# A recommender's attention over 200 history rows: more embedding rows fetched by address, asked four steps ahead, and VectorE empties the first layer's PSUM

## The chip, the cores and the metric

The kernel runs on one core of a Trainium2 chip. The metric is device time in microseconds for one launch. Engines carry the profile's names: PE (TensorE), DVE (VectorE), ACT (ScalarE), POOL (GpSimd) and SP (SyncE); SPq, ACTq and POOLq are their queues, which issue DMAs.

## What is computed

The reference, cut to what matters (B = 16384 samples, L = 200 history entries, embeddings of D = 64 floats, tables of 100,000 rows, hidden width A = 36):

```python
it = i_emb[item]                       # [B, 64]
h = i_emb[hist]                        # [200, B, 64]
feat = concatenate([h, itb, h - itb, h * itb], axis=-1)
a = dice(feat @ au_W1 + au_b1, au_alpha, axis=1)   # moments over B, for each l
w = a @ au_W2 + au_b2
cur = sum(w * h, axis=0)
z = concatenate([u, it, c, cur])       # then a small head of three layers
```

`dice(x)` is `x * (p + alpha * (1 - p))` with `p` the sigmoid of `x` normalized by its mean and variance over the batch. So for each of 200 values of l, 16,384 rows of 256 bytes are fetched from a table in HBM, put through a small layer, and the layer's output can be gated only when its moments over the whole batch are known.

## The kernel before

**Tiles and steps.** The batch is 128 tiles of P = 128 samples. Eight columns of TD = 16 tiles make up one l; one column is one step, so the main part has 1,600 steps, numbered k = 8 l + c. The loop body (L580) holds 90 l written out and runs twice; the last 20 l and the head follow. All engine orders are written out by hand (`manual_schedule`): each engine executes its instructions in program order and waits on semaphores.

**How rows come.** Most tiles come by `gather` (L123): one indirect DMA issued by POOL fetches 128 rows by a column of ids in SBUF. Three tiles of each l, the last tile of columns 3, 5 and 7 (`SIDES`, L27), come "by address" instead: their ids are loaded into one partition (`load_addresses`, L136), scaled to byte offsets by DVE (`scale_addresses`, L139), and SP and ACT fetch them into registers, up to LOAD = 28 at a time (L326), and issue one 256-byte DMA for each row (`row_by_address`, L290) into one of BUFS = 6 side buffers. These row DMAs are called asks here. The 384 rows of an l are spread evenly over its eight steps, 24 on SP and 24 on ACT in each (`shares`, L304; `ask_hist`, L343). When a column is due, DVE waits on the buffer's semaphore, clears it (`await_rows`, L349) and copies the tile to its place in the column (`place`, L384; `place_tile`, L390). Gathered columns go into a ring of ROWS = 5 buffers, so POOL can run up to four steps ahead of DVE.

**One step** (`step`, L435) works on several columns at once: rows of column k are fetched (L358); column k-1 is turned, by four DVE transposes into hT (L149), and multiplied on PE into the PSUM tiles ph and px (`turn`, L406; `product`, L411, where DVE forms hm = ph * itT); column k-2 leaves px for xs with the bias added (`hidden`, L376, on ACT), and DVE takes its batch statistics (`measure`, L379); column k-9 is gated on ACT (`gate`, L364: pg from xs, with the scale and shift of its l), DVE multiplies pg by xs into y and PE forms wb (`weights`, L368), and DVE weighs hT by it and adds to curT (`weigh`, L372). Every eighth step the moments of an l are finished (`moments`, L415) right after its last column's statistics, ahead of that step's transposes. All of DVE's work of a step stands in one order: statistics and moments, place, transposes, measure, hm, y, wb, curT. PE's order is ph, px, px from hm, wb. px has one buffer: the next step's px matmuls wait until hidden has read it.

**ACT's queue** in a step: hidden, the asks (24, in one load), gate. **SP's queue**: the id loads (L131), the address load at column 2 of an l for the next l, and its 24 asks in each step; it has nothing else and runs ahead until a side buffer or an address table isn't free. Addresses are scaled by DVE at column 4.

**Before the loop** (L526 to L577) the item rows are gathered, category rows are picked by matmuls, and the head's weights are loaded by SP at c = 2 (`head_weights`, L242), with a wait of DVE for them. **After it** (L664 on) user rows are fetched while the last columns are weighed, two of their tiles by address, and the head's layers follow.

Of the kernel before, what the change touches and what calls it, by code (L numbers as in the profile page):

```python
# [15 lines left out]
P = 128  # L16
# [5 lines left out]
LPB = 90  # L22
ROWS = 5
# [3 lines left out]
SIDES = (3, 5, 7)  # L27
BUFS = 6
# [7 lines left out]
def din_kernel(  # L36
# [80 lines left out]
    addrs = make("addrs", 2 * S + 1, NS * P, dt=I32)  # L117
    addr = [addrs[i * S : i * S + 1] for i in range(3)]
# [160 lines left out]
    keys = {}  # L279

    def tiles_by_address(l):

        return l * NS, range(NS)
# [30 lines left out]
    def ask(queue, runs, first, tiles, at, table):  # L314
# [6 lines left out]
        for r0, end in runs:  # L321
            while r0 < end:
                many = end - r0
                while place_of(r0 + many - 1) != place_of(r0) + many - 1:
                    many -= 1
                _, loaded = nc.values_load_multi_w_load_instructions(  # L326
                    at[:, place_of(r0) : place_of(r0) + many],
                    engines=(engine,), min_val=0, max_val=ROW * (table.shape[0] - 1),
                    skip_runtime_bounds_check_because="scale_addresses holds the address to the table",
                )  # L330
                for r, a in enumerate(loaded, r0):
                    m, p = first + r // P, r % P
                    key = keys.setdefault(m, f"rows{next(serial)}")
                    dma = row_by_address(
                        queue,
                        side[m % BUFS].bitcast(U8)[p : p + 1],
                        flat[ds(a, ROW)].rearrange("(o d) -> o d", o=1),
                    ).then_inc(landed[m % BUFS], 16)
# [4 lines left out]
    def ask_hist(k, queue, some):  # L343
        l, s = divmod(k, ND)
        first, tiles = tiles_by_address(l)
        runs = shares(len(tiles) * P // ND, s, SPLIT)[queue]
        ask(queue, runs[some], first, tiles, addr[l % 3], i_emb)

    def await_rows(m):  # L349
        if m in keys:  # L350
            fence = nc.vector.wait_ge(landed[m % BUFS], 16 * P)
            tc.declare_fence(fence.ins, group=keys.pop(m))
            nc.vector.sem_clear(landed[m % BUFS])

    def has_side(k):
        return k % ND in SIDES

    def fetch(k):  # L358
        l, c = divmod(k, ND)
        for n in range(TD - has_side(k)):  # L360
            j = column(c, n)
            gather(rows[k % ROWS], idx[l % IDX][:, j : j + 1], n, i_emb)
# [13 lines left out]
    def hidden(k):  # L376
        nc.scalar.activation(xs[k % XR], px, AF.Identity, bias=au_bias)  # L377
# [57 lines left out]
    def step(k, last=None, weighed=()):  # L435
# [30 lines left out]
    def steps(l0, n, end, then=None):  # L466
        for k in range(n * ND):
# [58 lines left out]
    with tc.manual_schedule():  # L526
# [19 lines left out]
        for c in range(ND + 1):  # L546
# [8 lines left out]
            if c == 0:  # L555
                attention_weights()
                load_hist_ids(0, 0)
                load_addresses(0, r_hist[0:1])
                scale_addresses(0)
            if c == 2:  # L560
# [9 lines left out]
        for t in (*hT[:SPREAD], *side, curT[0], rows[-1 % ROWS]):  # L570
# [5 lines left out]
        for c in range(1, 2 * ND):  # L576
            nc.vector.tensor_copy(stats[-1 % 3][:, c, :], stats[-1 % 3][:, 0, :])  # L577

    if BODY:
        with tc.For_i(0, BODY, LPB) as l0:  # L580
# [83 lines left out]
    with tc.manual_schedule():  # L664
# [4 lines left out]
        tiles = [SIDES.index(c) for c in (3, 5) if c in SIDES]  # L669
# [131 lines left out]
```

## Time and profile before

| | |
|---|---|
| Median of 3 runs | 31,650.93 us (31,650.28 to 31,652.98) |
| The profiled execution | 31,646.96 us, its span 31,645.1 us |
| Mean granted TensorE clock | 0.806 |
| Busy share of the span | POOL 75%, PE 66%, DVE 49%, PE weight loads 27%, ACT 12% |
| Asks for history rows | 38,400 on SP, 38,400 on ACT |
| Gathers for history rows | 25,000 on POOL |

How to read it: busy shares count instructions of the engine itself. A queue that only issues DMAs, or fetches addresses into registers, isn't busy by this count; such work is seen in the timelines, as rows of SPq and ACTq, and in a line's or tile's own view. In a group's row the first number after the bar is busy time, then the mean length of one in ns, then the idle time ahead of these instructions and what ended most of it. A row of a timeline has its start, its length (both in us) and how many instructions it merges; in brackets stands the idle time ahead of it. A row of the stage table has the stretch, its length, busy time and count of PE, PE's weight loads, DVE, ACT and POOL, then granted clock, DMA share and GB/s.

### The profile page before, as it was taken

How to read it: one execution, taken by the hardware profiler on the slowest of the kernel's cores; microseconds unless marked ns; L12 is line 12 of the kernel's file. 1: busy time of each engine (PE TensorE's matmuls, PEld its weight loads, DVE VectorE, ACT ScalarE, POOL GpSimd, SP SyncE). 2: the span in 40 equal slices, each digit the busy share in tenths (PEclk: the TensorE clock that was granted, in tenths of full speed). 3: DMA queues.
4: the chain of work that ended last, by engine and by line, in shares of the span. 5: the costliest groups of instructions: out<-in, count | busy, mean ns of one | idle time of the engine just before them, and what ended most of it. 6: DMA issues, size and time to landing. Idle time of an engine off the chain costs nothing.

```text
span 31645.1 us, 223489 instructions
## 1 busy us (share of the span) xinstructions
PE 20823.3 (66%) x39536; PEld 8584.9 (27%) x39536; DVE 15548.7 (49%) x21275; ACT 3817.4 (12%) x3322; POOL 23853.6 (75%) x25259
## 2 busy tenths in 40 slices
PE   6666666666666666666666666666666666666666
PEld 2222222222222222222222222222222222222222
DVE  5444444444444444444444444444444444444445
ACT  1111111111111111111111111111111111111111
POOL 7777777777777777777777777777777777777776
PEclk8888788887888888888788888887878788887888
DMA  2111111111111111111111111111111111111111
GB/s 44 28 28 28 28 28 28 28 28 28 28 28 28 28 28 28 28 28 28 28 28 28 28 28 28 28 28 28 28 28 28 28 28 28 28 28 28 28 28 30
DMA packets 1008142, 894.16 MB, mean 28 GB/s; under 512 B 597358, under 2 KB 597559, under 8 KB 1006695
## 3 DMA queue, kind: packets, MB, share of 16 engines
q0 software_dynamic: 808128, 829.14, 15.0%
q1 hardware_dynamic: 114362, 27.92, 0.4%
q10 hardware_dynamic: 84205, 22.70, 0.3%
q14 instruction: 1136, 9.31, 0.1%
q8 instruction: 311, 5.10, 0.1%
HBM read 873.48 MB, written 4.39 MB: 28 GB/s over the span
## 4 chain that ended last, share of the span: by engine, by line
POOL 30%; issue 11%; PE 6%; DMA 5%; DVE 2%; DVEq 0%; ACT 0%; POOLq 0%; ACTq 0%
POOL rows L124 30%; DMA rows<-in_L_rec_i_emb,idx 5%; PE px L154 3%; PE ph L154 2%; PE wb L154 2%; DVE hT L149 1%; DVE wb L373 1%; DVE curT L374 0%; DVE st L382 0%; DVEq L149 0%; DVE mv L418 0%; DVE rows L392 0%; DVE addrs L141 0%; POOLq L124 0%; PE pg L154 0%
## 5 line engine op out<-in xcount | busy, mean ns | idle before, releaser
L124 POOL DMA_INDIRECT rows<-in_L_rec_i_emb,idx x25000 | 23591.6, 944 | 7633.1 <-issue 7166.6
L154 PE MATMUL ph<-hT,unit 128*128 128x512 f32 x6404 | 5969.6, 1088 | 10697.5 <-DVE hT L149 10697.5
L373 DVE SCALAR_TENSOR_TENSOR wb<-wb,au_bias,hT 128x1024 f32<-128x1024 f32 x1609 | 2079.7, 1293 | 10748.4 <-PE wb L154 10748.4
L149 DVE STREAM_TRANSPOSE hT<-rows 64x512 f32<-64x512 f32 x6404 | 4518.5, 706 | 2971.8 <-DMA rows<-in_L_rec_i_emb,idx 2529.3
L154 PEld LDWEIGHTS ph<-hT,unit 128*128 128x128 f32 x6404 | 1796.1, 311 | 13756.3 <-DVE hT L149 13561.4
L154 PE MATMUL px<-hT,blk_h 128*128 128x512 f32 x6404 | 4065.3, 723 | 0.0
L377 ACT ACTIVATE xs<-px,au_bias 128x1024 f32<-128x1024 f32 x1602 | 1784.1, 1114 | 14492.6 <-PE wb L154 14492.5
L366 ACT ACTIVATE pg<-xs,sh,rs 128x1024 f32<-128x1024 f32 x1609 | 1943.3, 1208 | 12967.9 <-issue 10092.6
L154 PE MATMUL px<-itT,blk_i 128*128 128x512 f32 x6404 | 3382.0, 610 | 0.0
L154 PE MATMUL wb<-y,blk_p 128*128 128x512 f32 x6436 | 3291.1, 593 | 11.3 <-DVE y L369 11.3
L154 PE MATMUL wb<-xs,blk_x 128*128 128x512 f32 x6436 | 3289.2, 593 | 2.6 <-DVE curT L374 2.6
L154 PE MATMUL px<-hm,blk_m 128*128 128x512 f32 x6408 | 3011.3, 592 | 0.0
L412 DVE TENSOR_TENSOR hm<-ph,itT 128x1024 f32<-128x1024 f32 x1601 | 1960.4, 1224 | 1934.9 <-PE ph L154 1934.9
L154 PEld LDWEIGHTS px<-hT,blk_h 128*128 128x128 f32 x6404 | 1627.8, 254 | 2406.1 <-issue 2304.8
L382 DVE BATCH_NORM_STATS2 st<-xs 128x6 f32<-128x512 f32 x3204 | 2058.4, 684 | 44.5 <-ACT pg L366 0.3
L369 DVE TENSOR_TENSOR y<-pg,xs 128x1024 f32<-128x1024 f32 x1609 | 1955.7, 1215 | 85.0 <-ACT pg L366 82.9
L374 DVE TENSOR_TENSOR curT<-wb,curT 128x1024 f32<-128x1024 f32 x1609 | 1969.8, 1224 | 54.8
L154 PEld LDWEIGHTS px<-itT,blk_i 128*128 128x128 f32 x6404 | 1404.8, 219 | 2000.0 <-issue 2000.0
L154 PEld LDWEIGHTS wb<-y,blk_p 128*128 128x128 f32 x6436 | 1224.5, 190 | 1551.8 <-issue 1537.2
L154 PEld LDWEIGHTS wb<-xs,blk_x 128*128 128x128 f32 x6436 | 1224.3, 190 | 1541.4 <-issue 1538.0
L154 PEld LDWEIGHTS px<-hm,blk_m 128*128 128x128 f32 x6408 | 1219.0, 190 | 1531.4 <-issue 1524.2
L124 POOL DMA_INDIRECT rows<-in_L_rec_i_emb,ids x125 | 139.7, 1118 | 39.6 <-issue 37.2
(180 smaller groups left out, 1779.3 us busy)
## 6 DMA issues: line engine op xcount, KB each, us to landing
side<-in_L_rec_i_emb SPq DMA_DIRECT2D x38400, 0.2 KB
side<-in_L_rec_i_emb ACTq DMA_DIRECT2D x38400, 0.2 KB
rows<-in_L_rec_i_emb,idx POOLq DMA_INDIRECT x25000, 2.5
idx<-in_r_hist SPq DMA_DIRECT2D x200, 62.5 KB
hT<-cs ACTq DMA_DIRECT2D x16, 500.0 KB
ucT<-catT SPq DMA_DIRECT2D x8, 512.0 KB
side<-in_L_rec_u_emb SPq DMA_DIRECT2D x256, 0.2 KB
addrs<-in_r_hist SPq DMA_DIRECT2D x200, 1.5 KB
```

Of the source, the lines that this page charges most:

```text
L124: nc.gpsimd.indirect_dma_start(out=dst[:, n, :], out_offset=None, in_=table, in_offset=bass.IndirectOffsetOnAxis(ap=ids, axis=0),)
L149: nc.vector.transpose(by_tile(dst[ts(e, D)], i)[:, n], of[ts(i, D), n, ts(e, S)])
L154: nc.tensor.matmul(dst[:, ts(i, CH)], lhsT, rhs[:, ts(i, CH)], start=(first and j == 0), stop=(last and j == len(pairs) - 1), skip_group_c ...
L366: nc.scalar.activation(pg, xs[k % XR], AF.Sigmoid, bias=shifts[i], scale=rstds[i])
L369: nc.vector.tensor_mul(y, pg, xs[k % XR])
L373: nc.vector.scalar_tensor_tensor(wb, wb, au_bias2, hT[k % LAG], ALU.add, ALU.mult)
L374: nc.vector.tensor_add(curT[k % ND], wb, curT[k % ND])
L377: nc.scalar.activation(xs[k % XR], px, AF.Identity, bias=au_bias)
L382: nc.vector.bn_stats(stats[l % 3][:, 2 * c + i, :], xs[k % XR][:, ts(i, CH)])
L412: nc.vector.tensor_mul(hm, ph, itT[k % ND])
```

## The change

1. `SIDES` becomes (1, 2, 3, 4, 5, 6, 7), with column 2 only in each fifth l: 6 tiles by address in four l, 7 in the fifth, 6.2 on average. SP and ACT each ask 48 rows a step (two loads of 24), 56 in the fifth l (two of 28). Of the other four l, column 2's last tile is gathered, with ids from a small tile `sidx` of its own.
2. Side buffers go from 6 to 9. The rows that were asked in step k are now those of step k + 4 (`LEAD`), over the ends of the loop body too: at its end and before it, DVE waits until what has been asked of the next l has landed (`hold`). The address load moves from column 2 to 0, the scaling from 4 to 3 (896 addresses instead of 384). The first four steps' rows, 384, are asked on SP before the loop, at c = 1, and the loads of user ids and head weights move behind them, to c = 8.
3. `hidden` moves from ACT to DVE. In DVE's order it stands first in a step, behind the curT of the step before, ahead of moments, place and transposes. ACT's queue in a step is now: a load of 24 or 28 asks, gate, a second load of 24 or 28.

```diff
+LEAD = 4
-SIDES = (3, 5, 7)
-BUFS = 6
+SIDES = (1, 2, 3, 4, 5, 6, 7)
+SOMETIMES = 2
+EACH = 5
+BUFS = 9
...
+    def load_side_ids(i, l):
+        j = column(SOMETIMES, TD - 1)
+        nc.sync.dma_start(sidx[i], r_hist[ds(l, 1), j * P : (j + 1) * P].rearrange("l p -> p l"))
...
-        return l * NS, range(NS)
+        first = l * (NS - 1) + l // EACH
+        return first, [j for j, c in enumerate(SIDES) if has_side(l * ND + c)]
...
+    def land(m):
+        fence = nc.vector.wait_ge(landed[m % BUFS], 16 * asked[m])
+        tc.declare_fence(fence.ins, group=keys.pop(m))
...
     def await_rows(m):
         if m in keys:
-            fence = nc.vector.wait_ge(landed[m % BUFS], 16 * P)
-            tc.declare_fence(fence.ins, group=keys.pop(m))
-            nc.vector.sem_clear(landed[m % BUFS])
+            land(m)
+        elif m not in held:
+            return
+        held.discard(m)
+        asked.pop(m)
+        nc.vector.sem_clear(landed[m % BUFS])
+
+    def hold(l):
...
+        for m in sorted(keys):
+            land(m)
+            held.add(m)
 
     def has_side(k):
-        return k % ND in SIDES
+        l, c = divmod(k, ND)
+        return c in SIDES and (c != SOMETIMES or l % EACH == EACH - 1)
...
     def hidden(k):
-        nc.scalar.activation(xs[k % XR], px, AF.Identity, bias=au_bias)
+        nc.vector.tensor_scalar(xs[k % XR], px, au_bias, None, ALU.add)
...
-        if has(k):
-            ask_hist(k, 0, slice(None))
-            ask_hist(k, 1, slice(0, 1))
+        asks = has(k) and k + LEAD < until
+        if asks:
+            ask_hist(k + LEAD, 0, slice(None))
+            ask_hist(k + LEAD, 1, slice(0, 1))
         if k - LAG not in weighed:
             gate(k - LAG)
-        if has(k):
-            ask_hist(k, 1, slice(1, None))
+        if asks:
+            ask_hist(k + LEAD, 1, slice(1, None))
...
-            if c == 2 and (l + 1 < end or then is not None):
+                if (l + 1) % EACH < EACH - 1:
+                    load_side_ids((l + 1) % IDX, l0 + l + 1)
+            if c == 0 and (l + 1 < end or then is not None):
                 load_addresses((l + 1) % 3, r_hist[ds(l0 + l + 1, 1)] if l + 1 < end else then)
-            if c == 4 and (l + 1 < end or then is not None):
+            if c == 3 and (l + 1 < end or then is not None):
                 scale_addresses((l + 1) % 3, i_emb if l + 1 < end else u_emb)
-            step(k)
+            step(k, until=end * ND)
...
-            if c == 2:
+            if c == 1:
+                for j in range(LEAD):
+                    for share in range(2):
+                        ask_hist(j, share, slice(None), 0)
+            if c == ND:
                 nc.sync.dma_start(ids[1], columns(r_user))
                 load_all_ids(1, r_user)
                 head_weights()
...
                 await_rows(tiles_by_address(LPB)[0] - 1)
+                hold(LPB)
```

More of the change, by code (lines that the diff above doesn't have):

```diff
@@ L117, in din_kernel @@
     addrs = make("addrs", 2 * S + 1, NS * P, dt=I32)
+    sidx = [make(f"sidx{i}", P, 1, dt=I32) for i in range(IDX)]
     addr = [addrs[i * S : i * S + 1] for i in range(3)]
@@ L361, in fetch @@
             j = column(c, n)
-            gather(rows[k % ROWS], idx[l % IDX][:, j : j + 1], n, i_emb)
+            ids = sidx[l % IDX] if j >= NC else idx[l % IDX][:, j : j + 1]
+            gather(rows[k % ROWS], ids, n, i_emb)
     def gate(k):
@@ L569, in din_kernel @@
             nc.scalar.copy(t, hm)
-        for t in (*hT[:SPREAD], *side, curT[0], rows[-1 % ROWS]):
+        for t in (*hT[:SPREAD], side[-1 % BUFS], curT[0], rows[-1 % ROWS]):
             nc.vector.memset(t, 0.0)
```

19 lines of the change are left out of this document (14 added, 5 removed).

## Prediction, made before the changed kernel was run

> **What bounds the kernel now.** I read the page first (span, busy times, costliest groups), then the stage table, then the timelines of single engines inside the loop.
>
> ```profile
> span 31645.1 us, 223489 instructions
> L124 POOL DMA_INDIRECT rows<-in_L_rec_i_emb,idx x25000 | 23591.6, 944 | 7633.1 <-issue 7166.6
> L149 DVE STREAM_TRANSPOSE hT<-rows 64x512 f32<-64x512 f32 x6404 | 4518.5, 706 | 2971.8 <-DMA rows<-in_L_rec_i_emb,idx 2529.3
> L373 DVE SCALAR_TENSOR_TENSOR wb<-wb,au_bias,hT 128x1024 f32<-128x1024 f32 x1609 | 2079.7, 1293 | 10748.4 <-PE wb L154 10748.4
> L377 ACT ACTIVATE xs<-px,au_bias 128x1024 f32<-128x1024 f32 x1602 | 1784.1, 1114 | 14492.6 <-PE wb L154 14492.5
> ```
> ```profile
> 185.00:14230.00 14045.00, 9236.00 (x17283) 3815.22 (x17281) 6892.02 (x9400) 1681.65 (x1450) 10613.84 (x11249) 0.80 0.16 28
> ```
>
> POOL is only 75% busy, but its idle time is "issue": it waits for nothing, each of its 25,000 gathers simply costs 944 ns and 0.3 us to the next. The stage table says it in one number: 11,249 gathers in 14,045 us, 1.2486 us each. POOL is the bound, without a pause. DVE is second: its transposes wait 2,529 us for rows.
>
> ```profile
> 200.08 2.88 DVE L149 STREAM_TRANSPOSE hT<-rows 64x512 f32<-64x512 f32 x4
> ...
> 10292.71 2.88 DVE L149 STREAM_TRANSPOSE hT<-rows 64x512 f32<-64x512 f32 x4 [1.46 <-DMA rows<-in_L_rec_i_emb,idx]
> ...
> 10297.99 1.23 DVE L412 TENSOR_TENSOR hm<-ph,itT 128x1024 f32<-128x1024 f32 x1 [1.07 <-PE ph L154]
> 10299.13 1.21 DVE L369 TENSOR_TENSOR y<-pg,xs 128x1024 f32<-128x1024 f32 x1
> 10306.57 1.29 DVE L373 SCALAR_TENSOR_TENSOR wb<-wb,au_bias,hT 128x1024 f32<-128x1024 f32 x1 [6.23 <-PE wb L154]
> 10307.90 1.23 DVE L374 TENSOR_TENSOR curT<-wb,curT 128x1024 f32<-128x1024 f32 x1
> 10313.19 2.88 DVE L149 STREAM_TRANSPOSE hT<-rows 64x512 f32<-64x512 f32 x4 [4.07 <-DMA rows<-in_L_rec_i_emb,idx]
> ...
> 31410.76 2.88 DVE L149 STREAM_TRANSPOSE hT<-rows 64x512 f32<-64x512 f32 x4 [1.30 <-DMA rows<-in_L_rec_i_emb,idx]
> ```
>
> One step is a chain through DVE and PE: transposes, PE's ph and px, hm, y, PE's wb, then wb and curT on DVE. In this step it ran from 10,292.71 to 10,309.13, 16.4 us; then DVE waited 4.07 us for rows. Over the loop: from the first transposes to the last, 31,210.7 us for 1,600 steps is 19.51 us a step; without the 2,971.8 us idle before transposes the chain is **17.65 us a step**. So DVE and PE have 1.86 us a step to spare, no more.
>
> **The change, part by part.** *Gathers.* An l has 128 tiles; 3, then 6.2 of them come by address. 3.2 x 200 = 640 gathers go, at 1.2486 us: 799 us. Were POOL still the bound, the span would be 31,645 - 799 = **30,846 us** (121.8 x 1.2486 / 8 = 19.01 us a step).
>
> *The DVE chain.* It gets the emptying of px, copies, and a longer scaling.
>
> ```profile
> L374 DVE TENSOR_TENSOR curT<-wb,curT 128x1024 f32<-128x1024 f32 x1609 | 1969.8, 1224 | 54.8
> L392 DVE COPY rows<-side 128x64 f32<-128x64 f32 x603 | 128.1, 212 | 12.0 <-PEq L580 4.9 <-DMA rows<-in_L_rec_i_emb,idx 3.0
> L710 DVE TENSOR_SCALAR y<-y,al1a,ala 128x1024 f32<-128x1024 f32 x1 | 0.8, 797 | 0.0
> ```
> ```profile
> L141 DVE TENSOR_SCALAR addrs<-addrs x201: 336/351/612, 42.5 to 31331.3; 1x384 int32<-1x384 int32 x101
> ```
> ```profile
> 199.79 0.18 DVE L392 COPY rows<-side 128x64 f32<-128x64 f32 x1
> ```
>
> - hidden: no row has a TENSOR_SCALAR out of PSUM. Nearest below is the 797 ns one in SBUF, nearest above the 1,293 ns one that reads and writes PSUM; hm, which also reads PSUM, takes 1.23 us, and the next starts 1.14 us after it. I take 1.15 us a step (0.75 to 1.3). It stands behind curT, in front of the next transposes, where no PE work covers it, so it counts in full. What it frees on ACT is spent on asks (below).
> - copies: one costs 0.29 us (199.79 to the transposes at 200.08); 3.2 more per l are 0.12 us a step. The wait and the clear of its semaphore are sequencer work, done while curT and hidden run. The copies wait 12.0 us in all today, so asking four steps ahead gains nothing there; it keeps the wait away while two queues work nearly all the time. If it failed, transposes, PE and all behind them would stand.
> - scaling: 896 instead of 384 addresses, at most 0.35 x 896/384 = 0.82 us; 0.05 us a step.
>
> Sum 17.65 + 1.15 + 0.12 + 0.05 = **18.97 us a step**, PE's part taken as it is (from transposes to wb 13.86 us in the step above; bounds below). Level with POOL's 19.01.
>
> [...]
>
> *ACT's queue.*
>
> ```profile
> L326 SPq TENSOR_LOAD <-addrs x1610: 553/1674/1929, 154.1 to 31497.1; - x179
> L326 ACTq TENSOR_LOAD <-addrs x1600: 1639/1667/1701, 192.0 to 31385.7; - x178
> ```
> ```profile
> 10072.88 1.11 ACT L377 ACTIVATE xs<-px,au_bias 128x1024 f32<-128x1024 f32 x1 [6.94 <-PE wb L154]
> 10074.60 7.37 ACTq L294 DMA_DIRECT2D side<-in_L_rec_i_emb  x24
> 10082.02 1.21 ACT L366 ACTIVATE pg<-xs,sh,rs 128x1024 f32<-128x1024 f32 x1 [8.03 <-issue]
> ...
> 10094.80 7.43 ACTq L294 DMA_DIRECT2D side<-in_L_rec_i_emb  x24
> ...
> 10112.75 7.65 ACTq L294 DMA_DIRECT2D side<-in_L_rec_i_emb  x24
> ...
> 10132.89 7.45 ACTq L294 DMA_DIRECT2D side<-in_L_rec_i_emb  x24
> ...
> 10150.74 7.43 ACTq L294 DMA_DIRECT2D side<-in_L_rec_i_emb  x24
> ```
>
> A load of 24 addresses and its 24 asks take 9.14 us where SP is quiet (10,072.88 to 10,082.02): 1.67 us to fetch the addresses, beside the ACTIVATE in front, then 0.31 us an ask. Where SP asks too, the 24 take 7.43, 7.65, 7.45 and 7.43 us in four loads running, 7.49 on average. From now on both ask nearly always, so I take 9.14 + 0.12 = 9.26 us. Two loads a step are 18.52 us, with the gate's 1.21 us beside a fetch. In an l of seven tiles loads have 28: 7.49 x 28/24 = 8.74, fetch up to 1.93, 0.1 between: 10.77, 21.5 a step. Mean over five l: (4 x 18.52 + 21.5)/5 = **19.12 us**, bounds 18.84 (9.14 a load) and 19.45 (all like the row of 7.65). That is the largest of the three.
>
> Nor is it even: y waits for its gate, which stands behind the step's first load. In the l of seven ACT falls 8 x 2.5 = 20 us behind DVE. Room: the gate may run from the end of one y to the start of the next, 18.97 - 1.22 - 1.21 = 16.5 us, and PE multiplies xs before it needs y; but column 0's gate also waits for the moments, late in that room. So beyond the mean 0 to 16 us are lost per five l; I take 4, since most of it fits in the room: 40 x 4 = 160 us.
>
> *SP's queue.*
>
> ```profile
> 10098.56 15.84 SPq L294 DMA_DIRECT2D side<-in_L_rec_i_emb  x48
> ...
> 10116.69 52.12 SPq L294 DMA_DIRECT2D side<-in_L_rec_i_emb  x144
> ```
>
> The first row is two loads of 24 with one fetch between; with the other fetch 17.5 us a step, with 28 20.2, mean 18.1. (The second is SP beside ACT's loads above.) What is moved in SP's queue: the asks run four steps ahead of the step that stands beside them; the address table is asked for at column 0 instead of 2 and scaled at 3 instead of 4, one step before the first ask that needs it; an id load of one column is new. SP waits for the scaling once an l, about 8 x 0.9 us that it has to spare, and holds up no one within a step: rows asked in step k are placed five steps later or more. DMA engines: the stage table's share is 0.16; the asks add 256 B each.
>
> *Prologue.* The first 384 asks go on SP ahead of the head's weights, for which DVE waits.
>
> ```profile
> 42.45 0.34 DVE L141 TENSOR_SCALAR addrs<-addrs 1x384 int32<-1x384 int32 x1
> ...
> 103.64 0.15 DVE L270 TENSOR_SCALAR al1b<-alb 128x1 f32<-128x1 f32 x1 [6.39 <-DMA alb<-in_L_rec_alpha]
> ...
> 185.87 2.87 DVE L149 STREAM_TRANSPOSE itT<-rows 64x512 f32<-64x512 f32 x4 [5.90 <-DMA rows<-in_L_rec_i_emb,side_ids]
> ```
> ```profile
> 68.31 0.34 SPq L250 DMA_DIRECT2D w1a<-in_L_rec_W  x1
> ```
>
> Asks from 42.8 us, 8 x 17.5 = 140 us, to 183; nine small loads of ids, 4 us by the 0.34 us of the SP row and a little between them; weights 103.64 - 68.31 = 35 us: to 222, where DVE stood at 186 before. DVE's loop starts 38 us later, at 238 us. POOL isn't held (four steps of buffers). The waits at the two loop ends (hold) come a step after the last ask: nothing, at most a step each.
>
> *Sum.* POOL 19.01, DVE 18.97, ACT 19.12, SP 18.1 us a step: ACT ends last, coupled to DVE through y. 238 + 1,600 x 19.12 + 160 + 234 (from the last transposes to the end, unchanged) = **31,224 us** of span. The profiled execution was 31,647 us beside a span of 31,645, the median 31,651: so 31,230.
>
> **Rivals.**
>
> 1. *DVE's chain ends last* (20%). PE's part of it swings with the granted clock: from transposes at 10,273.86 to wb at 10,288.60 are 14.74 us against 13.86 above. With 0.25 us more of that and hidden at 1.3: 238 + 1,600 x 19.37 + 160 + 234 = 31,624; half of that surplus gives 31,420. I put it at 31,400 to 31,588.
>
> ```profile
> 10273.86 2.88 DVE L149 STREAM_TRANSPOSE hT<-rows 64x512 f32<-64x512 f32 x4 [2.95 <-DMA rows<-in_L_rec_i_emb,idx]
> ...
> 10288.60 1.29 DVE L373 SCALAR_TENSOR_TENSOR wb<-wb,au_bias,hT 128x1024 f32<-128x1024 f32 x1 [7.09 <-PE wb L154]
> ```
>
> 2. *ACT's asks cost still more: slower* (15%). With the 160 us, the span of before is reached at (31,645 - 632)/1,600 = 19.38 us a step, that is at 9.39 us a load, 1.4% above 9.26. For it: the row of 7.65 us gives 9.42. Against it: three of four rows beside SP's asks are 7.43 to 7.45. At 9.6 us, 4% more, it is 19.88 us a step: 32,440 us. From there on nothing saved on POOL counts.
>
> [...]
>
> 4. *ACT asks as fast as with SP quiet* (7%): 18.84, POOL ends last, 30,850 to 30,950.
>
> 5. *The change saves POOL's time and gives all of it back* (7%): ACT or DVE at 19.3 to 19.45, within 0.2%.
>
> **How the numbers follow.** Forecast (30,950 to 31,400) 48%, rivals 20, 15, 3, 7, 7. A measurement tells 0.2% from no change, 63 us. Faster 0.48 + 0.20 + 0.03 + 0.07 = 0.78, same 0.07, slower 0.15. The range runs from POOL's floor, 30,850, to 31,670, leaving out rival 2, and a part of 4 and 5.
>
> **What would show it.** Right: 24,360 gathers at 944 ns; hidden at 1.1 to 1.25 us on DVE; transposes' wait for rows under 500 us in place of 2,529; POOL now waiting hundreds of us for DVE; y waiting for pg one to three thousand us, a part of it hidden behind PE, almost nothing before; runs of 24 asks at 7.5 us. Wrong: those runs at 7.7 and more (rival 2) or at 7.37 (4); gathers over 944 ns (3); copies waiting for rows by address, which I put at nothing.

## The result, and the profile after

| | before | after |
|---|---|---|
| Median | 31,651.43 us (4 runs, 31,650.28 to 31,652.98) | 34,503.26 us (4 runs, 34,468.95 to 34,592.75) |
| The profiled execution, its span | 31,646.96, 31,645.1 us | 34,468.95, 34,467.2 us |
| One step of the loop | 19.51 us | 21.24 us (rows in the section on the prediction's steps) |

The changed kernel takes 1.0905 times the time of before (95% interval 1.0884 to 1.0926): 9% slower, where 1.3% faster was forecast, and outside the range. One thing is needed to read the experiments: in most of them the kernel before, run beside them, itself took 41,676 to 41,804 us in place of 31,650, for a reason that no run shows, so those runs are compared only with each other.

The page of the changed kernel (line, engine, operation, count; busy time, mean ns; idle ahead of it and what ended most of that):

```profile
span 34467.2 us, 309701 instructions
...
L128 POOL DMA_INDIRECT rows<-in_L_rec_i_emb,idx x24200 | 22848.4, 944 | 10986.2 <-issue 5720.3
...
L157 DVE STREAM_TRANSPOSE hT<-rows 64x512 f32<-64x512 f32 x6404 | 4517.1, 705 | 3828.7 <-DMA rows<-in_L_rec_i_emb,idx 3431.9
...
L408 DVE TENSOR_SCALAR xs<-px,au_bias 128x1024 f32<-128x1024 f32 x1602 | 2043.0, 1275 | 9.3 <-PEq L620 4.2
L400 DVE TENSOR_TENSOR y<-pg,xs 128x1024 f32<-128x1024 f32 x1609 | 1955.5, 1215 | 100.0 <-ACT pg L397 99.8
...
L423 DVE COPY rows<-side 128x64 f32<-128x64 f32 x1243 | 262.4, 211 | 0.0
```

The gathers that were to go are gone, and one still takes 944 ns. But POOL's idle time rose from 7,633 to 10,986 us, and DVE's transposes wait 3,432 us for gathered rows, before 2,529. Everything that I had put on the path is quiet: y waits 99.8 us for its gate in the whole run, the copies of rows by address never wait, hidden takes 1.275 us. The kernel has become slower in the one place that the change relieved, the gathers. The waits say who stops POOL (total, times, longest):

```profile
POOL rows L128 <- issue: 5835.7, 18043, 7.4
POOL rows L128 <- DMA rows<-in_L_rec_i_emb,idx: 5131.5, 6460, 5.1
...
DVE hT L157 <- DMA rows<-in_L_rec_i_emb,idx: 3431.9, 974, 14.8
```

POOL waited 6,460 times for an earlier gather to land, up to 5.1 us, 5,131 us in all. The trace says which one: the gathers use eight semaphores in turn (119 to 126), and each waits for the landing of the gather eight before it. At the pace of before that leaves a gather some 9 us after its own end (7 x 1.249 + 0.3). Before, POOL's wait was 0.3 us at most, its usual pause from one gather to the next:

```profile
POOL rows L124 <- DMA rows<-in_L_rec_i_emb,idx: 336.0, 1102, 0.3
```

In the chain that ended last, DMA now has the largest share, 27% (before 5%):

```profile
DMA 27%; POOL 18%; issue 8%; PE 1%; DVE 0%; ACT 0%; POOLq 0%; DVEq 0%; ACTq 0%
```

Next the stage table inside the loop (stretch, length, PE, weight loads, DVE, ACT and POOL with counts, granted clock, DMA share, GB/s), then the DMA queues of before and of after (packets, MB, the time that the packets took as a share of 16 engines' span; q0 is POOL's, q1 SP's, q10 ACT's):

```profile
1000.00:15000.00 14000.00, 8400.83 (x15859) 3474.07 (x15858) 7152.54 (x9496) 796.91 (x660) 9492.85 (x10056) 0.79 0.22 26
```
```profile
q0 software_dynamic: 808128, 829.14, 15.0%
q1 hardware_dynamic: 114362, 27.92, 0.4%
q10 hardware_dynamic: 84205, 22.70, 0.3%
```
```profile
q0 software_dynamic: 787648, 808.13, 14.3%
q1 hardware_dynamic: 220858, 38.71, 3.7%
q10 hardware_dynamic: 166893, 33.30, 3.3%
```

A gather now comes every 14,000 / 10,056 = 1.392 us, before every 1.249. The DMA share went from 0.16 to 0.22 although the core moves fewer GB/s (26, before 28). That looks harmless as a mean of 16 engines; but 0.06 x 16 = 0.96 is about one whole engine. The queues say whose it is: SP's and ACT's packets took 0.7% of 16 engines before, 0.11 of one engine; now 7.0%, which is 1.12 of one engine. It can be more than 1 because these times overlap: an ask leaves two packets, its 256 B and then 4 B, which stand partly beside each other and beside those of the other queue. From 1,000 to 15,000 us at least one of them is under way for 63% of the time, before for 5%. The asks have doubled, the time of their packets has grown tenfold.

### The profile page after: what moved, and what is told of

The parts are those of the page before. It is cut to its first block, busy times and chain, and to the rows that moved or that the text cites. A ratio compares the mean times of both kernels' runs of the same rounds, so it can differ in the third digit from the quotient of the medians.

```text
span 34467.2 us, 309701 instructions
## 1 busy us (share of the span) xinstructions
PE 20677.7 (60%) x39536; PEld 8530.5 (25%) x39536; DVE 17595.9 (51%) x23512; ACT 2029.2 (6%) x1717; POOL 23258.1 (67%) x24619
## 4 chain that ended last, share of the span: by engine, by line
DMA 27%; POOL 18%; issue 8%; PE 1%; DVE 0%; ACT 0%; POOLq 0%; DVEq 0%; ACTq 0%
DMA rows<-in_L_rec_i_emb,idx 27%; POOL rows L128 18%; PE px L162 0%; PE ph L162 0%; PE wb L162 0%; DVE hT L157 0%; DVE wb L404 0%; PE px L677 0%; DMA rows<-in_L_rec_u_emb,ids 0%; DVE xs L408 0%; PE pg L162 0%; DVE ucT L157 0%; DVE curT L405 0%; POOLq L128 0%; ACT hT L695 0%
## 5 line engine op out<-in xcount | busy, mean ns | idle before, releaser
L128 POOL DMA_INDIRECT rows<-in_L_rec_i_emb,idx x24200 | 22848.4, 944 | 10986.2 <-issue 5720.3
L157 DVE STREAM_TRANSPOSE hT<-rows 64x512 f32<-64x512 f32 x6404 | 4517.1, 705 | 3828.7 <-DMA rows<-in_L_rec_i_emb,idx 3431.9
L162 PE MATMUL px<-hT,blk_h 128*128 128x512 f32 x6404 | 3929.6, 700 | 0.0
L408 DVE TENSOR_SCALAR xs<-px,au_bias 128x1024 f32<-128x1024 f32 x1602 | 2043.0, 1275 | 9.3 <-PEq L620 4.2
L400 DVE TENSOR_TENSOR y<-pg,xs 128x1024 f32<-128x1024 f32 x1609 | 1955.5, 1215 | 100.0 <-ACT pg L397 99.8
L423 DVE COPY rows<-side 128x64 f32<-128x64 f32 x1243 | 262.4, 211 | 0.0
```

Of the source, the lines that this page charges most:

```text
L128: nc.gpsimd.indirect_dma_start(out=dst[:, n, :], out_offset=None, in_=table, in_offset=bass.IndirectOffsetOnAxis(ap=ids, axis=0),)
L157: nc.vector.transpose(by_tile(dst[ts(e, D)], i)[:, n], of[ts(i, D), n, ts(e, S)])
L162: nc.tensor.matmul(dst[:, ts(i, CH)], lhsT, rhs[:, ts(i, CH)], start=(first and j == 0), stop=(last and j == len(pairs) - 1), skip_group_c ...
L400: nc.vector.tensor_mul(y, pg, xs[k % XR])
L408: nc.vector.tensor_scalar(xs[k % XR], px, au_bias, None, ALU.add)
L423: nc.vector.tensor_copy(rows[k % ROWS][:, TD - 1], side[m % BUFS])
```

## The theories

**One DMA engine.** The theory, deduced from the traces, is that every ask, from SP's queue or from ACT's, goes through one and the same of the 16 DMA engines, which also carries a sixteenth of every gather, and that the changed kernel fills it. The trace's records of single packets don't name a packet's engine, and that a gather's 16 packets go to the 16 engines, one each, is an assumption. Five things in the records, which the views above only sum up, speak for the theory:

- An ask's packet of 256 B took 15 ns before, on either queue, 99 in 100 at most 18 ns. After, the medians are 175 ns (SP) and 173 (ACT), and 57% and 54% take over 100 ns.
- From its issue to the start of its packet, an ask of ACT waited 0.91 us before (median; 99 in 100 under 1.26), after 5.5 us (12.1); SP's asks 0.89 and 6.0. Both queues are late together: between their mean waits in stretches of 20 us the correlation is 0.98.
- Only a sixteenth of each gather is late. Its 128 rows are 16 packets of 2 KB, and it raises its semaphore sixteen times. The fifteenth of these landings comes 1.50 us after the end of POOL's instruction (median; before 1.46), the sixteenth after 8.2 us (before 1.5). The sixteenth's delay goes with the wait of the asks (correlation 0.98), the fifteenth's doesn't (0.1).
- The asks' packets pause while one gather packet is served. Of the pauses over 60 ns, 46% begin and end within 20 ns of the beginning and end of one gather packet. With the pauses shifted by 5 us it is 3%, which is chance.
- In 365 stretches of 50 us in which every ask waited over 2 us, 50 us = a x asks + b x gathers is best met by a = 0.177, b = 0.220 us; in two more traces of the same kernel by 0.182 and 0.188, and by 0.182 and 0.184. With 99.2 asks and 15.2 gathers a step: 17.6 + 3.3 = **20.9 us** (20.9 by the other two as well), against 19.0 that POOL needs and 21.24 measured. By the same numbers before stood at 48 x 0.177 + 15.6 x 0.22 = 11.9.

That 20.9 comes near 21.24 is no test by itself, since the stretches are the kernel's own; the test is another number of asks. One lies in the same trace: in the eight steps in which an l of seven tiles is asked for, 112 rows are asked a step, else 96. By a and b these eight steps take 185 and 163 us, by POOL alone 152 both times. Measured from DVE's transposes they take 185 to 189 us, and 162 to 171 (means by the l's place in the five). How the 20.9 us divide between asks and gathers is less sure than their sum: by the packets' time, 63% of a step is 0.135 us an ask, and the rest is up to 0.5 us a gather.

**Rivals.** *Hidden disturbs*: VectorE's new 1,275 ns instruction holds up POOL or lengthens the chain. *A cost in proportion*: every further ask costs something by its issue or its bytes, with no point at which something is full. *Bytes*: the engine, or HBM, pays by the byte and not by the ask.

## Experiments

**The kernel itself again, and five tiles.** The edit of the five-tile version, beside the changed kernel (the ids of column 2 and `sidx` are then not needed; in the first l of the loop body the 80 asks a step are split 96 and 64, so that no tile is half asked at its end):

```diff
-SIDES = (1, 2, 3, 4, 5, 6, 7)
-SOMETIMES = 2
+SIDES = (1, 3, 4, 5, 7)
+SOMETIMES = None
...
-        first = l * (NS - 1) + l // EACH
+        first = l * NS
```

> The changed kernel itself, unchanged. On a chip where the kernel before takes 31,650 us it takes 34,500 us (measured). On the chip of the runs so far, where the kernel before takes 41,770 us, every queue stands still for stretches and an ask there takes SP more than twice as long: theory 'one DMA engine' has no place there, since the asks come too slowly to fill it, and the kernel's time is set by SP's queue, which 80,481 instructions at 0.586 us (as in the run with hidden on ACT) put at 47,000 us.

> The changed kernel itself once more, beside the five-tile version in one go. Where the kernel before takes 31,650 us: 34,500 us. Where it takes 41,750: as the versions with hidden on ACT (47,080 to 47,310) and with asks of 64 bytes (46,810 to 46,930) it is set by SP's asks, which there take 0.586 us an instruction: 46,800 to 47,300 us. If it then is far below both, hidden on ACT or the size of the asks did cost something.

> Five tiles by address in every l. Where the kernel before takes 31,650 us, theory 'one DMA engine': 17.5 us a step on that engine, below POOL's 19.20, 31,050 to 31,400 us; rival 'each ask costs in proportion' 33,400; rival 'hidden disturbs' 33,500 and more. Where the kernel before takes 41,750 us: 42,000 to 42,200, as measured three times, which tells nothing of these.

Measured: the changed kernel 34,520.27 us beside 31,647.91 for before, and 34,596.10 beside 31,651.88. **Five tiles took 31,175.67 us** beside the same 31,651.88, 0.985 of it (one run each, so without an interval; the runs of before that took about 31,650 us lie between 31,647.9 and 31,653.0). Its page with the queues, its stage table, and two rows of DVE's timeline:

```profile
span 31173.9 us, 277486 instructions
...
q0 software_dynamic: 795328, 816.01, 12.2%
q1 hardware_dynamic: 166522, 34.62, 1.8%
q10 hardware_dynamic: 135597, 29.31, 1.5%
...
L128 POOL DMA_INDIRECT rows<-in_L_rec_i_emb,idx x24600 | 23223.6, 944 | 7531.6 <-issue 7320.5
...
L157 DVE STREAM_TRANSPOSE hT<-rows 64x512 f32<-64x512 f32 x6404 | 4515.8, 705 | 665.2 <-DMA rows<-in_L_rec_i_emb,idx 416.5
...
L411 DVE TENSOR_SCALAR xs<-px,au_bias 128x1024 f32<-128x1024 f32 x1602 | 2042.9, 1275 | 6.7 <-PEq L620 1.5
...
L403 DVE TENSOR_TENSOR y<-pg,xs 128x1024 f32<-128x1024 f32 x1609 | 1955.2, 1215 | 5.2 <-ACT pg L400 5.2
```
```profile
1000.00:15000.00 14000.00, 9281.21 (x17504) 3839.25 (x17503) 7872.95 (x10414) 882.78 (x731) 10571.59 (x11198) 0.82 0.16 28
```

```profile
237.25 2.88 DVE L157 STREAM_TRANSPOSE hT<-rows 64x512 f32<-64x512 f32 x4
...
30940.29 2.88 DVE L157 STREAM_TRANSPOSE hT<-rows 64x512 f32<-64x512 f32 x4
```

A gather comes every 14,000 / 11,198 = 1.250 us, as before. POOL is the bound again, without a pause. By the two rows of DVE's timeline, the first transposes of the loop and the last, an l takes (30,940.29 - 237.25) / 200 = 153.5 us; POOL needs 123 x 1.2486 = 153.6. Hidden on DVE takes the same 1,275 ns as in the changed kernel, so it isn't what slowed that. Nor is there a cost in proportion: 80 of 99.2 asks cost nothing, the last 19 cost 3,300 us. The engine is busy here but not always full: the queues show 3.3% x 16 = 0.53 of an engine for the asks and 0.12 for the gathers' sixteenth; 22% to 25% of the asks' packets take over 100 ns, and ACT's asks wait 0.97 us in the median, 4.0 at 99 in 100. Backlogs come and go. The sixteenth landing of a gather comes 3.1 us after its end in the median and 8.5 us at most, inside the 9 us that eight semaphores leave, and POOL waits 0.3 us at most for a landing (191.5 us in all).

**Everything of the change but the tiles, and other single parts.** Beside these runs the kernel before took 41,687 to 41,791 us, and they tell less than they were meant to. Three tiles (the rest of the edit as with five):

```diff
-SIDES = (1, 2, 3, 4, 5, 6, 7)
+SIDES = (3, 5, 7)
```

> All of the change except the number of tiles: three tiles by address in each l as before (48 asks a step), asked four steps ahead, nine side buffers, hidden on DVE. Theory 'one DMA engine': 48 x 0.177 + 15.6 x 0.22 = 11.9 us a step on that engine, no backlog; POOL is the bound as before at 15.625 gathers of 1.2486 us a step, 31,600 to 31,750 us, with asks landing in about 1 us. Rival 'hidden disturbs': most of the 2,850 us of loss stay, above 33,500 us. Rival 'asking ahead over two queues, the waits at the loop's ends or the nine buffers cost': above 32,000 us.

> All of the change except the number of tiles: three tiles by address in each l as before (48 asks a step), asked four steps ahead, nine side buffers, hidden on DVE. Theory 'one DMA engine': 48 x 0.177 + 15.6 x 0.22 = 11.9 us a step there, POOL the bound as before, 31,600 to 31,750 us. Rival 'hidden disturbs': most of the 2,850 us of loss stay, above 33,500 us. Rival 'asking ahead, the waits at the loop's ends or the nine buffers cost': above 32,000 us.

The five tiles again:

> The changed kernel with five tiles by address in every l (80 asks a step) in place of 6.2. Theory 'one DMA engine': 80 x 0.177 + 15.4 x 0.22 = 17.5 us a step on that engine, below POOL's 15.375 x 1.2486 = 19.20 us, so no lasting backlog: 1,600 x 19.20 + about 225 before the loop + 234 after = 31,180 us, 31,050 to 31,400, faster than both kernels. Rival 'each ask costs in proportion' (SP's and ACT's issue, or the ask's bytes, with no point at which something is full): of the 3,650 us between the changed kernel and its POOL floor of 30,850, two tiles of 3.2 would cost 2,280 beside a floor of 31,150: 33,400 us. Rival 'hidden disturbs': 33,500 us and more.

> The changed kernel with five tiles by address in every l in place of 6.2, once more, since on the chip of the first time the kernel before took 41,758 us and every queue stood still for stretches, which hides the question. On a chip where the kernel before takes 31,650 us, theory 'one DMA engine' expects 80 x 0.177 + 15.4 x 0.22 = 17.5 us a step on that engine, below POOL's 19.20, and 31,050 to 31,400 us. Rival 'each ask costs in proportion': 33,400 us. Rival 'hidden disturbs': 33,500 us and more.

> The changed kernel with five tiles by address in every l (80 asks a step) in place of 6.2. Theory 'one DMA engine': 80 x 0.177 + 15.4 x 0.22 = 17.5 us a step on that engine, below POOL's 15.375 x 1.2486 = 19.20 us, no lasting backlog: 1,600 x 19.20 + about 225 before the loop + 234 after = 31,180 us, 31,050 to 31,400, faster than both kernels. Rival 'each ask costs in proportion' (its issue or its bytes, with no point at which something is full): of the 3,650 us between the changed kernel and POOL's floor of 30,850, two tiles of 3.2 would cost 2,280 beside a floor of 31,150: 33,400 us. Rival 'hidden disturbs': 33,500 us and more.

> The changed kernel with five tiles by address in every l (80 asks a step) in place of 6.2, where the kernel before takes 31,650 us. Theory 'one DMA engine' (every ask, from either queue, goes through one and the same of the 16 DMA engines, which also carries a sixteenth of every gather): 80 x 0.177 + 15.4 x 0.22 = 17.5 us a step on that engine, below POOL's 15.375 x 1.2486 = 19.20 us, no lasting backlog: 1,600 x 19.20 + about 225 before the loop + 234 after = 31,180 us, 31,050 to 31,400, faster than both kernels. Rival 'each ask costs in proportion' (its issue or its bytes, with no point at which something is full): of the 3,650 us between the changed kernel and POOL's floor of 30,850, two tiles of 3.2 would cost 2,280 beside a floor of 31,150: 33,400 us. Rival 'hidden disturbs' (hidden on DVE holds up POOL or lengthens the chain): 33,500 us and more.

Hidden put back on ACT:

```diff
 def hidden(k):
-    nc.vector.tensor_scalar(xs[k % XR], px, au_bias, None, ALU.add)
+    nc.scalar.activation(xs[k % XR], px, AF.Identity, bias=au_bias)
```

> The changed kernel, with hidden put back on ACT (in ACT's order first in a step, ahead of the asks). Theory 'one DMA engine': every ask, from SP's queue or from ACT's, goes through one and the same of the 16 DMA engines, which also carries a sixteenth of every gather; in the changed kernel's trace that engine is full (an ask takes it about 0.18 us, a gather's share about 0.22: 99.2 x 0.177 + 15.2 x 0.22 = 20.9 us a step, above POOL's 19.0). Then who empties px makes no difference: 34,500 us, within 300, and DVE still waits thousands of us for gathered rows. Rival 'hidden disturbs' (hidden on DVE, at 1,275 ns, holds up POOL or lengthens the chain): the loss goes, 31,000 to 31,700 us. Rival 'ACT is too full': ACT's queue gets 1.1 us a step more, so slower still, 35,000 and more, with y waiting thousands of us for pg.

> The changed kernel with hidden put back on ACT, once more for the same reason. On a chip where the kernel before takes 31,650 us, theory 'one DMA engine': 34,500 us within 300, with thousands of us of waits for gathered rows. Rival 'hidden disturbs': 31,000 to 31,700 us. Rival 'ACT is too full': 35,000 us and more, with y waiting thousands of us for pg.

> The changed kernel with hidden put back on ACT, where the kernel before takes 31,650 us. Theory 'one DMA engine' (every ask, from either queue, goes through one and the same of the 16 DMA engines, which also carries a sixteenth of every gather; 99.2 asks x 0.177 + 15.2 gathers x 0.22 = 20.9 us a step there, above POOL's 19.0): 34,500 us within 300, DVE still waiting thousands of us for gathered rows. Rival 'hidden disturbs' (hidden on DVE holds up POOL or lengthens the chain): the loss goes, 31,000 to 31,700 us. Rival 'ACT is too full': 1.1 us a step more there, 35,000 us and more, with y waiting thousands of us for pg.

Asks of 64 bytes:

```diff
-                        side[m % BUFS].bitcast(U8)[p : p + 1],
-                        flat[ds(a, ROW)].rearrange("(o d) -> o d", o=1),
+                        side[m % BUFS].bitcast(U8)[p : p + 1, :64],
+                        flat[ds(a, 64)].rearrange("(o d) -> o d", o=1),
...
-        nc.vector.tensor_copy(rows[k % ROWS][:, TD - 1], side[m % BUFS])
+        nc.vector.tensor_copy(rows[k % ROWS][:, TD - 1, : 16], side[m % BUFS][:, : 16])
```

> The changed kernel, but each ask fetches only the first 64 of a row's 256 bytes, and the copy to the column takes only those 16 elements: three quarters of each row by address are left out. The number of asks, loads of addresses and waits is unchanged. Theory 'one DMA engine, a fixed cost for each ask': 34,300 to 34,600 us. Rival 'bytes' (the engine, or HBM, pays by the byte): an ask costs a quarter, 99.2 x 0.044 + 3.3 = 7.7 us a step, the backlog goes, POOL is the bound at 19.0 us a step and the time is 31,000 to 31,300 us. Between the two, a fixed part and a part by the byte: in between.

> The changed kernel, but each ask fetches only the first 64 of a row's 256 bytes, and the copy takes only those 16 elements: three quarters of each row by address are left out. Number of asks, address loads and waits unchanged. Theory 'one DMA engine' with a fixed cost for each ask: 34,300 to 34,600 us. Rival 'bytes' (the engine, or HBM, pays by the byte): an ask costs a quarter, 99.2 x 0.044 + 3.3 = 7.7 us a step, no backlog, POOL the bound: 31,000 to 31,300 us. In between: a fixed part and one by the byte.

And five tiles with half the l in the loop body:

```diff
-LPB = 90
+LPB = 45
```

> The changed kernel with five tiles by address in every l (80 asks a step) in place of 6.2, and 45 l instead of 90 written out in the loop body, which runs four times (half the program; two more turns of the loop, each at most a step of 19 us). Where the kernel before takes 31,650 us, theory 'one DMA engine' (every ask, from either queue, goes through one and the same of the 16 DMA engines, which also carries a sixteenth of every gather): 80 x 0.177 + 15.4 x 0.22 = 17.5 us a step on that engine, below POOL's 15.375 x 1.2486 = 19.20 us, no lasting backlog: 31,180 us, with the two turns up to 31,220; 31,050 to 31,400 in all, faster than both kernels. Rival 'each ask costs in proportion' (its issue or its bytes, with no point at which something is full): of the 3,650 us between the changed kernel and POOL's floor of 30,850, two tiles of 3.2 would cost 2,280 beside a floor of 31,150: 33,400 us. Rival 'hidden disturbs' (hidden on DVE holds up POOL or lengthens the chain): 33,500 us and more.

| | us | before beside it |
|---|---|---|
| three tiles | 41,855 (10 runs; ratio 1.0024, 1.0014 to 1.0033); again 41,634 | 41,758; 41,687 |
| five tiles | 42,167 (ratio 1.0092, 1.0075 to 1.0109); again 42,111 (1.0082, 1.0064 to 1.0099), 42,076 (1.0094, 1.0077 to 1.0110), 42,030; with 45 l 42,220 | 41,758; 41,791; 41,687; 41,693; 41,707 |
| hidden on ACT, 6.2 tiles | 47,307; again 47,216, 47,076 | 41,758; 41,791; 41,687 |
| asks of 64 bytes, 6.2 tiles | 46,934; again 46,815 | 41,758; 41,687 |

Here the engine, by its packets, isn't full. Of the version with hidden on ACT (47,076 us), the queues and the chain:

```profile
q1 hardware_dynamic: 220858, 38.71, 0.4%
q10 hardware_dynamic: 166893, 33.30, 0.3%
...
SPq 26%; issue 18%; ACTq 6%; DVE 2%; PE 2%; another core or an unknown queue 1%; ACT 1%; DMA 0%; DVEq 0%; POOL 0%; POOLq 0%
```

The asks take 0.7% of 16 engines, as little as before, and the chain runs through SP's queue. In these runs 6.2 tiles are slow because SP can't ask fast enough (80 asks in 45.98 us, 0.57 us each, in the run of 47,307 us), so they don't test the theory. Three tiles, with asking ahead, nine buffers and hidden on DVE, took between 0.2% more and 0.1% less than before: no change. With 45 l in the loop body the time stayed at 42,220 us.

**The transfers by themselves.** A kernel with nothing but gathers and asks, in eight stretches. Each row says whether POOL gathers, which queues ask (0 is SP, 1 is ACT), how many addresses a load has, the bytes of an ask, and in how many parts it is asked for:

```python
    PHASES = (
        (True, (), 28, ROW, 1),
        (False, (0, 1), 28, ROW, 1),
        (True, (0,), 28, ROW, 1),
        (True, (0, 1), 8, ROW, 1),
        (True, (0, 1), 14, ROW, 1),
        (True, (0, 1), 28, ROW, 1),
        (True, (0, 1), 28, ROW // 4, 1),
        (True, (0, 1), 28, ROW, 2),
    )
```

> Only the disputed transfers, the whole computation left out: eight stretches after each other, each with 208 gathers of 128 rows on POOL (none in the second) and 512 asks on a queue. (1) gathers alone; (2) SP and ACT ask in loads of 28, no gathers; (3) gathers and SP; (4) gathers and both queues in loads of 8, (5) of 14, (6) of 28; (7) as 6 with asks of 64 bytes; (8) as 6 with each ask cut in two packets of 128 bytes. With 1.7 us a load and 0.3 an ask, asks come at 5.5 a us in (2) and (6) to (8), 2.8 in (3), 3.9 in (4), 4.7 in (5). Theory 'one DMA engine' (all asks and a sixteenth of each gather go through one engine, which needs 0.177 us for an ask and 0.22 for a gather's share): full at 4.7 asks a us beside gathers every 1.25 us. So gathers keep 1.25 us in (1), (3), (4); (5) stands at the edge; in (6) and (7) ask packets take over 100 ns in place of 15 and POOL's gathers get slower; (2), 5.5 x 0.177 = 0.97, just holds; (8) is the worst. Rival 'bytes': (7) is as good as (4). Rival 'hidden, DVE or the chain': none of this is here, so no stretch slows. Rival 'issue': asks come slower in the stretches with both queues, packets stay at 15 ns.

Before took 41,804 us beside it. SP's queue in it, the whole second and third stretch, then the third up to its last gather and from there, then the sixth up to its last gather:

```profile
250.49 220.20 SPq L115 DMA_DIRECT2D side<-in_L_rec_i_emb  x512
...
477.59 390.01 SPq L115 DMA_DIRECT2D side<-in_L_rec_i_emb  x512
```
```profile
477.59 261.04 SPq L115 DMA_DIRECT2D side<-in_L_rec_i_emb  x215
```
```profile
739.34 128.26 SPq L115 DMA_DIRECT2D side<-in_L_rec_i_emb  x297
```
```profile
1728.79 261.58 SPq L115 DMA_DIRECT2D side<-in_L_rec_i_emb  x199
```

Without gathers, SP and ACT both ask 512 in 220 us, 4.65 a us together, and packets stay at 15 ns (0.84 of the engine by 0.18 us an ask). Beside gathers SP alone comes to one ask in 1.21 us, with the fetches, and to one in 0.43 us as soon as the gathers end; whether ACT asks too makes little difference (1.31, and 1.26 on ACT). So in this run the issue on SP and ACT is slower beside POOL's gathers, and stretches 4 to 8 never reached the rates that they were meant to have: 1.5 to 1.6 asks a us. The packets stayed at 15 ns (8 in the seventh stretch). In the eighth an ask remained one packet of 256 B. Of the engine the run tells one thing: 4.65 asks a us are as many as the changed kernel's (99.2 / 21.24 = 4.67), and without gathers they leave no backlog. At that rate asks alone didn't fill the engine; in the changed kernel as many asks stood beside gathers.

**No arithmetic, and three kinds of asks.** The first drops the bodies of hidden, measure, moments, gate, weights, weigh and product and the matmuls of turn; the second changes the asks by l:

```diff
-        ask(queue, runs[some], first, tiles, addr[l % 3], i_emb)
+        size, each = ((ROW, 1), (ROW // 4, 1), (ROW, 2))[l % LPB // 30]
+        ask(queue, runs[some], first, tiles, addr[l % 3], i_emb, size, each)
```

> The changed kernel's main part with all of its arithmetic left out: gathers, address loads and scaling, asks four steps ahead, the copies and the transposes stay, PE's matmuls, hidden, statistics, moments, gate, y, wb and curT are gone. Theory 'one DMA engine': the engine still needs 99.2 x 0.177 + 15.2 x 0.22 = 20.9 us a step, so 33,600 to 34,600 us, DVE waiting for gathered rows. Every rival that needs hidden, DVE's chain, PE or the gate: POOL alone is left, 19.01 us a step, 30,750 to 31,000 us.

> The changed kernel with three kinds of asks, by l of the loop body: l 0 to 29 as they are; l 30 to 59 fetch only the first 64 of a row's 256 bytes; of l 60 to 89 every second ask is left out (all addresses are still loaded, the waits count what was asked). So three quarters of the rows by address in the second third, and half of those rows in the last, are left out. Read by the time of an l in each third, at the usual pace. Theory 'one DMA engine' with a fixed cost of an ask: 171 us in the first third as in the changed kernel, 171 in the second, 153 in the last (49.6 x 0.177 + 3.3 = 12 us a step there; POOL at 121.8 x 1.2486 = 152 us and DVE's chain at 8 x 18.97 = 152 set the pace): 60 x (171 + 171 + 153) + 20 x 171 + 472 = 33,590 us. Rival 'bytes': 171, 154, 153, 32,570 us in all. Rival 'cost by issue': the last third lies halfway between 171 and 152, and the second at 171. At the slower pace (before at 41,750 us) the thirds are set by SP's and ACT's issue and tell nothing of the engine.

They took 47,419 us beside 41,804 for before, and 45,019 beside 41,676. Without any arithmetic the kernel is no faster than the version with hidden on ACT (47,076 to 47,307 above), and DVE's copies wait 28,979 us for asked rows, so in these runs the asks alone set the time:

```profile
SPq 34%; issue 19%; ACTq 1%; DMA 1%; another core or an unknown queue 0%; DVE 0%; PE 0%; ACT 0%; DVEq 0%
```

In the other, the stage table of the three thirds of the first turn of the loop:

```profile
1000.00:7000.00 6000.00, 2695.44 (x5052) 1109.90 (x5050) 2274.11 (x3038) 253.57 (x210) 3022.22 (x3204) 0.72 0.09 19
7500.00:13500.00 6000.00, 2667.98 (x4992) 1100.91 (x4992) 2250.16 (x2995) 251.14 (x208) 2987.81 (x3167) 0.71 0.08 18
14200.00:20000.00 5800.00, 2925.59 (x5496) 1206.94 (x5496) 2475.94 (x3288) 275.31 (x228) 3289.74 (x3487) 0.74 0.09 21
```

With 121.8 gathers an l: 228, 231 and 203 us. A quarter of the bytes saves nothing, half of the asks takes 26 us off. Here an ask costs by being issued, not by its bytes.

**What stays open.** Whether a shorter ask would cost the full engine less: the rival *bytes* was only tried where the engine isn't full. Why an ask costs 0.18 us there, though its packet can take 15 ns, isn't known. That it is one engine is read from the packet records; no experiment sent asks through another. Between 80 and 96 asks a step there is no measurement.

## Why the prediction was wrong, point by point

- *What bounds the kernel*: POOL was the bound, as read. With five tiles, at the same 1.25 us a gather, it still is.
- *DMA engines*: **the step that failed** is the sentence "DMA engines: the stage table's share is 0.16; the asks add 256 B each." It took a mean over 16 engines and counted bytes, and so put the engine at nothing in the sum. The asks were to be counted one by one, on one engine: 99.2 of them at 0.18 us and 15.2 sixteenths of gathers are 20.9 us a step by the fit, more than any term of the sum. The forecast's own sign of it was the transposes' wait for rows, 3,432 us in place of under 500. The share of before gave no warning by itself, since its packets took 15 ns; the 0.18 us could be estimated only from the trace of after, where the median packet took 175 ns.
- *Gathers*: 24,360 at 944 ns (24,200, and 160 with the ids of column 2), as said; but at 1.392 us from one to the next, since POOL waits for the late sixteenth. "POOL still the bound", 19.01 us a step, is what was lost.
- *DVE's chain*, forecast at 18.97 us: right within 1%. From DVE's timeline, the first transposes of the loop and the last ones:

```profile
239.84 2.88 DVE L157 STREAM_TRANSPOSE hT<-rows 64x512 f32<-64x512 f32 x4
...
34227.04 1.27 DVE L408 TENSOR_SCALAR xs<-px,au_bias 128x1024 f32<-128x1024 f32 x1
34228.23 0.18 DVE L423 COPY rows<-side 128x64 f32<-128x64 f32 x1
34228.45 2.88 DVE L157 STREAM_TRANSPOSE hT<-rows 64x512 f32<-64x512 f32 x4
```

  From 239.84 to 34,228.45 are 1,600 steps of 21.24 us. Without the transposes' idle time a step is 21.24 - 3,828.7 / 1,600 = 18.85 us. With five tiles (153.5 / 8 = 19.19 us a step) it is 19.19 - 665.2 / 1,600 = 18.77. Hidden was put at 1.15 us (0.75 to 1.3): it is 1.27 long, and the copy starts 1.19 us after it.
- *The copies and asking four steps ahead*, at nothing: right; the copies' idle time is 0.0, though an ask now waits 5.5 us.
- *ACT's queue*, forecast at 18.52 us a step of two loads of 24 (19.12 mean), which was to end last:

```profile
9999.40 1.21 ACT L397 ACTIVATE pg<-xs,sh,rs 128x1024 f32<-128x1024 f32 x1 [17.48 <-issue]
10001.22 16.98 ACTq L303 DMA_DIRECT2D side<-in_L_rec_i_emb  x48
10018.25 1.21 ACT L397 ACTIVATE pg<-xs,sh,rs 128x1024 f32<-128x1024 f32 x1 [17.65 <-issue]
10020.05 16.83 ACTq L303 DMA_DIRECT2D side<-in_L_rec_i_emb  x48
10036.93 1.21 ACT L397 ACTIVATE pg<-xs,sh,rs 128x1024 f32<-128x1024 f32 x1 [17.47 <-issue]
```

  Gate to gate 18.85 and 18.68 us: the size was about right, a little low. Over the run the median is 18.77 us with 48 asks and 21.60 with 56, a mean of 19.34, inside the bounds of 18.84 and 19.45. It never ended last, because the step grew to 21.24; whether it would have with an engine that isn't full, no run shows. The 160 us of coupling through y aren't there: 99.8 us of waits in all. ACT's issue doesn't slow down when the engine is full (0.302 us from ask to ask in the median, as before); the asks stand in the queue, so the full engine isn't seen in ACT's own timeline.
- *Prologue*: DVE's loop was to start at 238 us; its first transposes are at 239.84, its copy 0.2 us earlier.
- *The rivals*: number 2 had the side right and the reason wrong. A load on ACT cost 9.39 us (18.77 / 2) in place of 9.26, where that rival puts the pace of before; but ACT never ended last, so the loss isn't there. Numbers 1 and 4 are out: DVE's chain needs 18.85 us of the 21.24, and the asks didn't come faster. So is the chance of 3%, gathers over 944 ns: they stayed at 944 beside hidden. Number 5 named a loss in ACT or DVE; neither set the step. No rival had a DMA engine in it; the chance of 0.15 for slower stood on a mechanism that didn't make this loss.
- *The sum*: with five tiles, where the engine isn't full, the same terms give 1,600 x 19.20 + 225 + 234 = 31,180 us; it took 31,176. So close is partly luck: the loop began 12 us later than these 225, and its steps took 17 us less in all. The method held; one resource was missing from it.

## What to carry to other kernels

Count DMAs, and not only bytes, and count them for each DMA engine: here the one-row DMAs of two queues were late together (correlation 0.98), as if all of them ran through one of the 16. When transfers move from one path to another, the sum needs that engine as a term of its own, beside the engines that issue; a mean share of 0.16 hid it, and a share that rose by a sixteenth (0.06) while GB/s fell (28 to 26) was about one engine's worth here. Move a part first: here two more tiles by address gain 1.5%, and 3.2 lose 9%.

## What the runs showed of the hardware that was not expected

- An ask of 256 bytes cost about 0.18 us of one engine in the changed kernel (an estimate, by the fits, on the theory of one engine), where its packet took 175 ns in the median, and 15 ns in the kernel before; here a packet's time in a quiet trace was no measure of what the engine can take.
- A gather of which one landing in 16 is late stopped POOL, through the wait of the gather eight behind it (5,131 us in all): with a sixteenth landing at 8.2 us in the median, before 1.5, the distance between gathers went from 1.249 to 1.392 us, without any change in the gather's 944 ns.
- In the run of the transfers alone, SP's issue is slower beside gathers (one ask in 1.21 us, 0.43 without them). In the runs beside a kernel before of 41,687 us and more, the order of the versions isn't the same: five tiles lose 0.8% to 0.9% in place of gaining 1.5%.
